# An opening written out by hand: the second tile's first projections, its input, the value weights and the key copies take other places

## The chip, the core and the metric

The kernel runs on one core of one Trainium2 chip. The engines are PE (TensorE, matrix products), DVE (VectorE), ACT (ScalarE), POOL (GpSimd) and SP (SyncE, which here only gives out DMA orders). The metric is device time in microseconds (us); lower is better. A measurement is the median of several runs, and one execution beside them is profiled.

## The reference, cut to what matters

```python
# x: (64, 32, 512); W: 16 matrices 32 x 32, one chosen for each batch
x = x + einsum('bct,bcd->bdt', x, W[condition])
# attention: 32 query heads, 8 key/value heads, D = 128, 32 new tokens a batch
q = rope(rmsnorm(x @ Wq.T), pos)      # 64 x 32 x 32 x 128
k = rope(rmsnorm(x @ Wk.T), pos)      # 64 x 32 x 8 x 128
v = x @ Wv.T
# 16 pages of 32 cached keys and values a batch, valid up to cache_seqlens
k_all = concat([k_cache[block_table], k]); v_all = concat([v_cache[block_table], v])
probs = softmax(where(valid, q @ k_all.T * SCALE, -1e30))
x = x + (probs @ v_all) @ Wo.T
```

All of it is float32. Each batch has 512 cached keys and 32 new ones; four query heads share one key head.

## The kernel before, in words

**Tiles and steps.** A tile is 128 rows: four batches of 32 tokens. There are 16 tiles, and the heads are done in two halves (four key heads and sixteen query heads each), so there are 32 steps. A step has 16 slots: four batches by four parts j. A part is one pair of key heads (g) by one half of the cached keys: j = 0 and 1 are the two pairs on the first half, j = 2 and 3 the two pairs on the second (`part_of`).

**What a tile needs.** `x1_a` (L383) loads the tile of x on SP's queue, `x1_c` (L404) multiplies it by the block matrix of its four mix weights (`bds`) and adds, `x1_b` (L411) transposes the sum on PE and has ACT copy it into `x1t`. A projection (`project`, L467) is four matmuls 128 x 512 from `x1t` and one weight tile, each shown as two records in the profile; `finish` squares it on ACT (L479), takes the power -1/2 on POOL (L487, L488), and scales and rotates it on DVE (`norm_rope`, L496 to L514). `q_a` and `k_a` are projection and finish, `q_b` and `k_b` transpose the rows on PE (L527) and have ACT copy them into `q_ring` (L611). `v_product` is the value projection (`pp_v`), `v_copy` its copy to `vn`. `rot_tables` (L454 to L459) makes a tile's cosines and sines times the norm weights, `reduced` (L141 to L152, DVE) and `sines` (L157 to L159, ACT) make the angles.

**What a batch needs.** `load_k` (L312) loads one key half: eight pages of 64 KB, eight orders on SP (L321). The halves lie in a ring of three buffers (tag `k_t`), so the fourth half can be asked for only when nothing reads the first one any more. `head_keys` (L1006) copies the pair of heads of part j out of its half into `kh` (four buffers and some spare places), on ACT (L1015) or on DVE (L1017). `scores` (L1020) multiplies keys and queries on PE and takes the exponential on ACT (L1037). `fetch` (L345) gathers value rows by an indirect DMA of POOL into a ring of three (L354), `fill` scales them into `v_ring` on ACT (L366). `values` (L1081) multiplies probabilities and values on PE (L1089) and, after the second half, adds and divides on DVE (L1100 to L1103).

**The order.** The opening (L1223 to L1335) is written by hand for all engines: each engine does its work in program order there. It holds the first tile's projections, the first batches' keys and values, the mix and `k_a` of the second tile, and the first batch of attention. Then a plan gives to each step and slot the work that is done beside the scores and values (L1340 on); step 0 holds the second tile's four query projections in slots 4 to 7 and its value projection in slot 13 (L1393 to L1404). SP and PE follow the program's order throughout.

**SP's queue in the opening.** x of the first tile, all mix weights (`w_all`), query weights 0 and 1, both key halves of batch 0, the value weights, x of the second tile, the second tile's mix weights (`load_cond_weights`, L284: a register load of the four numbers and four small DMAs), query weights 3, both key halves of batch 1, six output-weight parts (L262), two halves of batch 2, and then in step 0 x and mix weights of the third tile, six more output-weight parts and the halves that follow. Key weights and query weights 2 come on POOL's queue.

The ring of key halves in `load_k`, and the copy out of it in `head_keys`:

```python
k_raw = kv.tile([P, HP, GH, PSIZE], F32, tag="k_t", name=..., bufs=3)
for j in range(HP):
    nc.sync.dma_start(k_raw[:, j, :, :]..., kt[hh, bass.ds(page[half * HP + j], 1)]...)
...
g, half = part_of(ba, j)
src = ba.k_raw[half][:, :, g : g + 2, :]...
```

Of the kernel before, what the change touches and what calls it, by code (L numbers as in the profile page):

```python
# [12 lines left out]
F32 = mybir.dt.float32  # L13
I32 = mybir.dt.int32
AF = mybir.ActivationFunctionType
# [5 lines left out]
P = 128  # L21
# [7 lines left out]
BT = P // S  # L29
# [31 lines left out]
def cond_resid_paged_attention_kernel(  # L61
# [68 lines left out]
    def positions():  # L130
        nc.vector.memset(half_pi, math.pi / 2)
        nc.vector.memset(minus_half, -0.5)
        nc.vector.tensor_copy(pos, lens_sb)
        nc.vector.tensor_scalar(pos, pos, row, None, ALU.add)

    def reduced(t0, tmp):

        t1 = t0 + TRIG
        n = TRIG * HD
        ang, turns, red = (tmp[:, i, :] for i in range(3))  # L140
        nc.vector.tensor_tensor(  # L141
            ang.rearrange("p (t f) -> p t f", f=HD),
            freq.unsqueeze(1).to_broadcast([P, TRIG, HD]),
            pos[:, t0:t1].unsqueeze(2).to_broadcast([P, TRIG, HD]),
            ALU.mult,
        )
        nc.vector.tensor_scalar(turns, ang, 1.0 / TWO_PI, ROUND, ALU.mult, ALU.add)
        nc.vector.tensor_scalar(turns, turns, ROUND, None, ALU.subtract)
        nc.vector.scalar_tensor_tensor(red, turns, -C1, ang, ALU.mult, ALU.add)
        nc.vector.scalar_tensor_tensor(red, turns, -C2, red, ALU.mult, ALU.add)  # L150
        nc.vector.scalar_tensor_tensor(red, turns, -C3, red, ALU.mult, ALU.add)
        nc.vector.tensor_scalar(red, red, PI_IN, -PI_IN, ALU.min, ALU.max)  # L152

    def sines(trig, tmp):

        _, turns, red = (tmp[:, i, :] for i in range(3))
        nc.scalar.activation(trig[:, 1, :, :].rearrange("p t f -> p (t f)"), red, AF.Sin)  # L157
        nc.scalar.activation(turns, red, AF.Abs)
        nc.scalar.activation(  # L159
            trig[:, 0, :, :].rearrange("p t f -> p (t f)"),  # L160
            turns,
            AF.Sin,
            bias=half_pi,
            scale=-1.0,
        )
# [37 lines left out]
    def steps_of(exact, pools):  # L203
# [43 lines left out]
        def load_w(kind, hh, g=0, part=slice(0, 4), eng=nc.sync):  # L247
            if kind == "q":
                src = wq[:, (hh * QH + g * REP) * D : (hh * QH + (g + 1) * REP) * D]
            elif kind == "o":  # L250
                src = wo[(hh * QH + g * REP) * D : (hh * QH + (g + 1) * REP) * D, :]
            else:
                src = (wk if kind == "k" else wv)[:, hh * GH * D : (hh + 1) * GH * D]
            if part.start == 0:
                wt[kind, hh, g] = wpool.tile(
                    [P, 4, 512], F32, tag=f"w{kind}{g}", name=f"w{kind}{g}_{hh}_{uid}"
                )
            t = wt[kind, hh, g]
            if kind == "o" and not exact:
                src = src.rearrange("(h j p) e -> h p j e", h=REP, p=S)  # L260
                for h in range(part.start, part.stop):
                    nc.sync.dma_start(t[h * S : (h + 1) * S, :, :], src[h])  # L262
                return
            eng.dma_start(t[:, part, :], src.rearrange("(c p) e -> p c e", p=P)[:, part, :])
# [9 lines left out]
        def conditions(t, kind):  # L274
            _, number = nc.values_load_multi_w_load_instructions(
                cond_row[:, t, :],
                engines=[kind],
                min_val=0,
                max_val=NCOND - 1,
                skip_runtime_bounds_check_because="a batch's condition is one of those there are",  # L280
            )
            return number

        def load_cond_weights(t, eng=nc.sync, kind=mybir.EngineType.SP):  # L284
            number = conditions(t, kind)
            for i in range(BT):
                blk = slice(i * S, (i + 1) * S)
                eng.dma_start(
                    bds[t % 2][blk, blk],
                    w_cond.rearrange("(n s) e -> n s e", s=S)[bass.ds(number[i], 1)].rearrange(  # L290
                        "o s e -> (o s) e"
                    ),
                )
# [89 lines left out]
        def x1_a(st):  # L383

            if st.pair is None:
                tag = "sums" if st.n and not exact else "acc"
                st.acc = work.tile([P, HID], F32, tag=tag, name=f"acc_{st.name}", bufs=2)
            else:
                i = st.n % 2
                if i == 0:  # L390
                    st.pair.read = work.tile(
                        [P, 2, HID], F32, tag="os", name=f"read_{st.name}", bufs=1
                    )
                st.acc = st.pair.read[:, i]
            src = acc_d[st.t] if st.hh else x[st.t * P : (st.t + 1) * P, :]
            nc.sync.dma_start(st.acc, src)
# [14 lines left out]
        def x1_b(st):  # L411
            if st.hh:
                return
            pm = ps_p.tile([P, KC, P], F32, tag="pp", name=f"px1t_{st.name}")
            for c in range(KC):
                nc.tensor.transpose(pm[:, c, :], st.acc[:, c * P : (c + 1) * P], ident)
            if st.pair is None:
                st.x1t = work.tile(
                    [P, KC, P], F32, tag="x1t" if exact else "u3", name=f"x1t_{st.name}", bufs=1
                )  # L420
            nc.scalar.copy(st.x1t, pm)
            if st.n or exact:
                kept.append(lambda: keep_x1t(st, nc.sync))
# [195 lines left out]
        def k_b(st):  # L619
            to_columns(st, GH)  # L620
# [14 lines left out]
        def q_a(st, g):  # L635
            name = f"q_{st.name}_{g}"
            finish(st, g, project(st, wt["q", st.hh, g], f"pp_{name}"), name, "q")

        def q_b(st, g):
            to_columns(st, g)  # L640
# [584 lines left out]
        w_all = work.tile([S, NCOND, S], F32, tag="pr", name="w_all", bufs=2)  # L1225
        nc.sync.dma_start(w_all, w_cond.rearrange("(n s) e -> s n e", s=S))
        load_w("q", 0, 0)
        load_w("q", 0, 1)
        nc.scalar.dma_start(lens_sb, lens)
        load_w("k", 0, eng=nc.gpsimd)  # L1230
# [7 lines left out]
        load_w("q", 0, 2, eng=nc.gpsimd)  # L1238
        batch = Batch(first, 0)
        batch.load_half()  # L1240
        batch.load_half()
        load_w("v", 0)
        x1_a(second)
        def keep_warm(n):
            warm = ps_p.tile([P, P], F32, tag="pp", name="warm")
            for _ in range(n):
                nc.tensor.matmul(warm, ident, ident, start=True, stop=True)

        keep_warm(WARM)
        number = conditions(0, mybir.EngineType.DVE)  # L1250
        for i in range(BT):
            blk = slice(i * S, (i + 1) * S)
            nc.vector.tensor_copy(
                bds[0][blk, blk], w_all[:, bass.ds(number[i], 1), :].rearrange("p o e -> p (o e)")
            )
        x1_c(first)
        keep_warm(4)
        x1_b(first)
        keep_warm(3)
        load_cond_weights(1)  # L1260
        load_w("q", 0, 3)
        later = Batch(first, 1)
        later.load_half()
        positions()
        trig = work.tile([P, 3, TRIG * HD], F32, tag="w1", name="trig0", bufs=1)
        reduced(0, trig)
# [2 lines left out]
        nc.vector.memset(vn_bufs[0][:, :, D : D + 1], 1.0)  # L1269
        nc.vector.memset(vn_bufs[1][:, :, D : D + 1], 1.0)  # L1270
        cached_rows(pages_at, lens_at)
        trig = work.tile([P, 3, TRIG * HD], F32, tag="w1", name="trig1", bufs=1)
        reduced(TRIG, trig)
        q_a(first, 0)
        sines(new_trig(TRIG), trig)
        table = small.tile([P, 1], F32, tag="rs", name="table")
        nc.scalar.activation(table, half_pi, AF.Exp)
        fetch(0, 0)
        fetch(0, 1)
        k_a(first)  # L1280
# [1 line left out]
        keep_x1t(first, nc.gpsimd)  # L1282
        for kind in "qk":
            keep_rot(first, kind, nc.gpsimd)
        q_a(first, 1)
        q_a(first, 2)
        fetch(0, RAW, tag="pn", bufs=1)
        q_b(first, 0)
        head_keys(batch, 0, nc.scalar)
        head_keys(batch, 2, nc.scalar)  # L1290
        k_b(first)
        head_keys(batch, 1, nc.scalar)
        later.load_half()
        head_keys(batch, 3, nc.scalar)
        for part in (0, 1, 2):
            load_parts(outputs, 0, part)
        after = Batch(first, 2)
        after.load_half()
        new = v_product(first)
        q_b(first, 1)  # L1300
        scores(batch, 0)
        for c in (0, 1):
            batch.fill(c)
            fetch(1, c)
        v_copy(first, new)
        x1_c(second)
        batch.fill(2)
        fetch(1, 2)
        batch.fill(3)
        scores(batch, 2)  # L1310
        values(batch, 0)
        q_a(first, 3)
        q_b(first, 2)
        x1_b(second)
        keep_x1(second, nc.gpsimd)
        head_keys(later, 0, nc.scalar)
        head_keys(later, 1, nc.scalar)
        after.load_half()
        rot_tables(second)
        k_a(second)  # L1320
        q_b(first, 3)
        scores(batch, 1)
        scores(batch, 3)
# [68 lines left out]
        by_vector = nc.vector.tensor_copy  # L1392
        for kind in "qk":  # L1393
            at(0, 5, lambda kind=kind: keep_rot(second, kind))
        for g in range(GH):
            at(0, 4 + g, lambda g=g: q_a(second, g))
        at(0, 12, lambda: to_columns(second, GH), lambda: to_columns(second, 0, by_vector))
        at(0, 13, lambda: v_a(second), lambda: to_columns(second, 1, by_vector))
# [302 lines left out]
```

## Time and profile before

| what | us |
|---|---|
| runs shown | 2078.98, 2082.15, 2083.43; median 2082.15 |
| profiled execution | 2077.26, of it the span 2075.5 |
| PE busy in the span | 2042.3 (98%) |
| PE busy from 0 to 40 / 40 to 120 / 120 to 2000 / 2000 to 2075 | 30.0 / 75.9 / 1872.1 / 64.3 |
| value projection of the first tile (PE) | starts 32.92 |
| key projection of the second tile (PE) | starts 49.07 |
| query projections 0 and 1 of the second tile (PE) | start 63.05 and 68.37 |
| value weights (SP) | ordered at 24.43 |
| key halves of batch 0 in, first to last packet | 15.8 to 21.4 and 21.4 to 28.3 |
| key halves of batch 1 | 35.3 to 39.7 and 39.7 to 45.8 |
| key halves of batch 2 | 54.0 to 57.7 and 57.7 to 63.0 |
| key halves of batch 3 | 74.5 to 79.2 and 79.3 to 86.5 |
| key halves of batch 4 | 86.8 to 92.2 and 92.2 to 96.3 |

The profile is of one execution, and its times count from the start of the span. A line of a timeline gives start, duration, engine, line of the kernel, operation, output and input by the program's names, shapes and a count, and in brackets the idle time of the engine just before it with what ended it. A line of the waits gives the engine's operation, what it waited for, the sum, the number of times and the longest. SPq lines are DMA orders: from the first of a group to the last. The span's PE clock is full, except in a few short stretches.

### The profile page before, as it was taken

The numbers are of one execution on the slowest core, as the hardware profiler recorded it, in microseconds if no ns is written. First come the engines' busy times: TensorE is split into PE (matmuls) and PEld (weight loads), VectorE is DVE, ScalarE is ACT, GpSimd is POOL, SyncE is SP. The second block draws the span as 40 slices with busy tenths as digits, with TensorE's granted clock in tenths as the row PEclk, the third lists the DMA queues.
The fourth block names the chain that finished last, engine by engine and source line by source line (L and its number), as shares of the span: only waits on it lengthen the run. The fifth ranks groups of instructions, "written<-read, shape, count | busy, mean of one in ns | idle before, by whom it ended". The sixth has DMA issues, their size and how long they took to land.

```text
span 2075.5 us, 45239 instructions
## 1 busy us (share of the span) xinstructions
PE 2042.3 (98%) x13428; PEld 1587.7 (76%) x13428; DVE 1630.7 (79%) x3532; ACT 958.4 (46%) x2707; POOL 991.2 (48%) x1122
## 2 busy tenths in 40 slices
PE   7999999999999999999999999999999999999998
PEld 4767667787887878878786677878878787787886
DVE  4555687988979789797997769889797987979744
ACT  4444354544545444544534445344454434545441
POOL 4354465545636465463544436355353544535331
PEclk9999999999999999999999999999999999999999
DMA  8767557667676676787767876676767667676672
GB/s 245 202 177 219 160 153 230 183 190 220 186 218 188 195 215 189 220 264 217 222 193 201 241 212 184 201 207 179 209 184 211 188 195 211 178 215 182 191 212 78
DMA packets 410255, 413.33 MB, mean 199 GB/s; under 512 B 58928, under 2 KB 325552, under 8 KB 410000
## 3 DMA queue, kind: packets, MB, share of 16 engines
q1 hardware_dynamic: 354096, 229.87, 39.1%
q0 software_dynamic: 55168, 180.27, 28.9%
q8 instruction: 109, 1.79, 0.4%
q14 instruction: 146, 1.20, 0.2%
q10 hardware_dynamic: 736, 0.21, 0.0%
HBM read 350.09 MB, written 60.03 MB: 198 GB/s over the span
## 4 chain that ended last, share of the span: by engine, by line
PE 80%; DVE 6%; DMA 6%; SPq 4%; issue 2%; POOL 1%; ACT 1%; DVEq 0%; ACTq 0%; POOLq 0%
PE ps_x L1026 18%; PE po_x L1089 18%; PE p_x L836 14%; PE pb_x L697 8%; PE pc_x L697 6%; PE pa_x L697 6%; PE pout_x L793 4%; SPq L321 3%; DMA k_t_x<-in_kt_dram 2%; PE pnv_x L1071 2%; PE pp_q_x L470 2%; PE psn_x L1047 1%; DMA q_ring_x<-heads_d 1%; PE pp_v_x L470 1%; DMA wq_x<-in_wq_dram 1%
## 5 line engine op out<-in xcount | busy, mean ns | idle before, releaser
L354 POOL DMA_INDIRECT raw_x<-in_vc_dram,v_row x512 | 548.3, 1071 | 639.8 <-ACT v_ring_x L366 518.4
L1037 ACT ACTIVATE pr_x<-ps_x 128x512 f32<-128x512 f32 x511 | 305.7, 598 | 779.1 <-PE ps_x L1026 774.1
L1089 PEld LDWEIGHTS po_x<-v_ring_x,pr_x 128*128 128x128 f32 x4088 | 522.9, 191 | 86.8 <-issue 66.2
L1026 PE MATMUL ps_x<-q_ring_x,kh_x 128*128 128x128 f32 x4088 | 546.4, 276 | 1.6 <-ACT q_ring_x L611 1.6
L1089 PE MATMUL po_x<-v_ring_x,pr_x 128*128 128x129 f32 x4088 | 543.5, 275 | 3.2 <-DVE nv_x L1100 2.8
L1026 PEld LDWEIGHTS ps_x<-q_ring_x,kh_x 128*128 128x128 f32 x4088 | 498.7, 192 | 13.8 <-issue 3.1
L366 ACT ACTIVATE v_ring_x<-raw_x,valid 128x512 f32<-128x512 f32 x512 | 342.7, 714 | 19.8 <-DMA raw_x<-in_vc_dram,v_row 19.2
L1017 DVE COPY kh_x<-k_t_x 128x512 f32<-128x512 f32 x506 | 219.8, 435 | 97.6 <-PE ps_x L1026 67.2
L544 POOL DMA_DIRECT2D heads_d<-rows_x x150 | 126.2, 842 | 280.8 <-DVE rows_x L540 215.9
L697 PE MATMUL pb_x<-t_x,early 128*128 128x512 f32 x504 | 238.2, 595 | 2.0 <-DVE u_x L713 1.1
L1100 DVE TENSOR_TENSOR nv_x<-po_x,nv_x 128x258 f32<-128x258 f32 x256 | 106.9, 417 | 100.7 <-PE po_x L1089 96.1
L836 PEld LDWEIGHTS p_x<-wo_x,ot_x 128*128 128x128 f32 x624 | 116.5, 190 | 62.3 <-issue 45.9
L488 POOL TENSOR_TENSOR rs_q_x<-ms_q_x,minus_half 128x4 f32<-128x4 f32 x128 | 158.8, 1241 | 10.7
L836 PE MATMUL p_x<-wo_x,ot_x 128*128 128x256 f32 x624 | 156.3, 380 | 0.1
L836 PE MATMUL p_x<-ts_x,ot_x 128*128 128x256 f32 x624 | 145.6, 380 | 0.7 <-DVE ts_x L911 0.7
L697 PEld LDWEIGHTS pb_x<-t_x,early 128*128 128x128 f32 x504 | 86.2, 191 | 64.8 <-issue 61.9
L836 PEld LDWEIGHTS p_x<-ts_x,ot_x 128*128 128x128 f32 x624 | 115.4, 190 | 25.3 <-issue 8.4
L1103 DVE TENSOR_TENSOR nv_x<-nv_x,rden 128x256 f32<-128x256 f32 x256 | 109.6, 428 | 8.7
L479 ACT ACTIVATE sq_q_x<-u_x 128x128 f32<-128x128 f32 x224 | 66.2, 298 | 94.0 <-DVE u_x L713 94.0
L697 PE MATMUL pc_x<-wq_x,early 128*128 128x512 f32 x224 | 105.4, 593 | 0.0
L697 PE MATMUL pa_x<-wq_x,early 128*128 128x512 f32 x224 | 105.4, 593 | 0.0
L514 DVE TENSOR_TENSOR rope_q_x<-rope_q_x,rs_q_x 128x512 f32<-128x512 f32 x120 | 82.3, 686 | 19.8 <-POOL rs_q_x L488 19.3
(203 smaller groups left out, 2612.0 us busy)
## 6 DMA issues: line engine op xcount, KB each, us to landing
k_t_x<-in_kt_dram SPq DMA_DIRECT2D x2048, 64.0 KB
heads_d<-rows_x POOLq DMA_DIRECT2D x150, 256.0 KB
q_ring_x<-heads_d SPq DMA_DIRECT2D x480, 80.0 KB
raw_x<-in_vc_dram,v_row POOLq DMA_INDIRECT x512
wo_x<-in_wo_dram SPq DMA_DIRECT2D x32, 256.0 KB
res_x<-acc_d SPq DMA_DIRECT2D x31, 256.0 KB
wq_x<-in_wq_dram SPq DMA_DIRECT2D x8, 512.0 KB
early<-x1t_d SPq DMA_DIRECT2D x16, 256.0 KB
```

Source lines behind the costliest of these rows:

```text
L354: nc.gpsimd.indirect_dma_start(out=raw.rearrange("p g d -> p (g d)"), out_offset=None, in_=vc, in_offset=bass.IndirectOffsetOnAxis(ap=v_ro ...
L366: nc.scalar.activation(v_ring[:, c, :, 0:D], raw, AF.Copy, scale=valid[:, b, c : c + 1])
L488: nc.gpsimd.tensor_tensor(rs, ms, minus_half, ALU.pow)
L544: nc.gpsimd.dma_start(heads_d[st.n][:, :, i, :].rearrange("k p c -> p k c"), part)
L697: nc.tensor.matmul(bank, pair.x[:, i, c, :], by[:, c * 512 : (c + 1) * 512], start=start and c == 0, stop=c == 1, skip_group_check=not start,)
L836: nc.tensor.matmul(to, left[:, i, :], right(i), start=start and i == 0, stop=i == QH // 2 - 1, skip_group_check=True,)
L1017: nc.vector.tensor_copy(to, src)
L1026: nc.tensor.matmul(ps[:, c, i, :], ba.k[j][:, i, c, :], queries(ba, g + i), start=True, stop=True,)
L1037: nc.scalar.activation(pr, ps, AF.Exp, scale=SCALE)
L1089: nc.tensor.matmul(ba.po[g][:, i, :], ba.pr[j][:, c, i, :], ba.v_t[:, 2 * half + c, g + i, :], start=(half == 0 and c == 0 and i == 0), st ...
L1100: nc.vector.tensor_tensor(t, ba.po[g], t, ALU.add)
L1103: nc.vector.tensor_tensor(t[:, :, 0:D], t[:, :, 0:D], rd.unsqueeze(2).to_broadcast([P, 2, D]), ALU.mult,)
```

## The change

- x of the second tile is ordered on SP between query weights 0 and 1 (was: after both key halves and the value weights).
- The value weights are ordered between the two key halves of batch 0 (was: after both).
- The second tile's mix weights are picked by DVE out of `w_all`, as the first tile's are (was: four DMAs of SP).
- The second tile's mix follows the first query projection on PE, its transposes the second; its `x1t` lies in a second buffer of the tag `acc` (was: `u3`).
- Its `rot_tables` and `keep_x1` on POOL, its `k_a` and its `q_a` 0 come ahead of the value projection, its `q_a` 1 after the fourth query projection of the first tile. The plan of step 0 keeps `q_a` 2 and 3 in slots 6 and 7.
- The angles of tiles 2 and 3 (`trig1`, now tag `nv`), their sines and the load of the exponential's table come after the second tile's `q_a` 0 (was: around the first tile's `q_a` 0).
- ACT's key copies of batch 0: j = 0 after the second tile's `k_a`; j = 2 after the first scores (was: next to j = 0); j = 1 after the fourth query projection (was: after `k_b`); j = 3 after the column copy of q2, `q_b(first, 2)` (was: after j = 1).

The order on PE after it: mix and x1t of the first tile, q0, the second tile's mix, k, q1, the second tile's x1t, q2, transposes of q0 and k, k of the second tile, transposes of q1, q0 of the second tile, v, scores j = 0, scores j = 2, values j = 0, q3, transposes of q2, q1 of the second tile, transposes of q3, scores j = 1 and j = 3, then as before, less the two projections.

```diff
--- before.py
+++ after.py
@@ -415,8 +415,13 @@
             for c in range(KC):
                 nc.tensor.transpose(pm[:, c, :], st.acc[:, c * P : (c + 1) * P], ident)
             if st.pair is None:
+                tag = "x1t" if exact else "acc" if st.n == 1 else "u3"
                 st.x1t = work.tile(
-                    [P, KC, P], F32, tag="x1t" if exact else "u3", name=f"x1t_{st.name}", bufs=1
+                    [P, KC, P],
+                    F32,
+                    tag=tag,
+                    name=f"x1t_{st.name}",
+                    bufs=2 if tag == "acc" else 1,
                 )
             nc.scalar.copy(st.x1t, pm)
             if st.n or exact:
@@ -1225,6 +1230,7 @@
         w_all = work.tile([S, NCOND, S], F32, tag="pr", name="w_all", bufs=2)
         nc.sync.dma_start(w_all, w_cond.rearrange("(n s) e -> s n e", s=S))
         load_w("q", 0, 0)
+        x1_a(second)
         load_w("q", 0, 1)
         nc.scalar.dma_start(lens_sb, lens)
         load_w("k", 0, eng=nc.gpsimd)
@@ -1238,29 +1244,33 @@
         load_w("q", 0, 2, eng=nc.gpsimd)
         batch = Batch(first, 0)
         batch.load_half()
+        load_w("v", 0)
         batch.load_half()
-        load_w("v", 0)
-        x1_a(second)
         def keep_warm(n):
             warm = ps_p.tile([P, P], F32, tag="pp", name="warm")
             for _ in range(n):
                 nc.tensor.matmul(warm, ident, ident, start=True, stop=True)
 
         keep_warm(WARM)
-        number = conditions(0, mybir.EngineType.DVE)
-        for i in range(BT):
-            blk = slice(i * S, (i + 1) * S)
-            nc.vector.tensor_copy(
-                bds[0][blk, blk], w_all[:, bass.ds(number[i], 1), :].rearrange("p o e -> p (o e)")
-            )
+
+        def pick_weights(t):
+            number = conditions(t, mybir.EngineType.DVE)
+            for i in range(BT):
+                blk = slice(i * S, (i + 1) * S)
+                nc.vector.tensor_copy(
+                    bds[t][blk, blk],
+                    w_all[:, bass.ds(number[i], 1), :].rearrange("p o e -> p (o e)"),
+                )
+
+        pick_weights(0)
         x1_c(first)
         keep_warm(4)
         x1_b(first)
         keep_warm(3)
-        load_cond_weights(1)
         load_w("q", 0, 3)
         later = Batch(first, 1)
         later.load_half()
+        pick_weights(1)
         positions()
         trig = work.tile([P, 3, TRIG * HD], F32, tag="w1", name="trig0", bufs=1)
         reduced(0, trig)
@@ -1269,12 +1279,9 @@
         nc.vector.memset(vn_bufs[0][:, :, D : D + 1], 1.0)
         nc.vector.memset(vn_bufs[1][:, :, D : D + 1], 1.0)
         cached_rows(pages_at, lens_at)
-        trig = work.tile([P, 3, TRIG * HD], F32, tag="w1", name="trig1", bufs=1)
-        reduced(TRIG, trig)
-        q_a(first, 0)
-        sines(new_trig(TRIG), trig)
-        table = small.tile([P, 1], F32, tag="rs", name="table")
-        nc.scalar.activation(table, half_pi, AF.Exp)
+        pp = project(first, wt["q", 0, 0], "pp_q_first")
+        x1_c(second)
+        finish(first, 0, pp, f"q_{first.name}_0", "q")
         fetch(0, 0)
         fetch(0, 1)
         k_a(first)
@@ -1282,42 +1289,49 @@
         keep_x1t(first, nc.gpsimd)
         for kind in "qk":
             keep_rot(first, kind, nc.gpsimd)
-        q_a(first, 1)
+        pp = project(first, wt["q", 0, 1], "pp_q_first_1")
+        x1_b(second)
+        finish(first, 1, pp, f"q_{first.name}_1", "q")
+        trig = work.tile([P, 3, TRIG * HD], F32, tag="nv", name="trig1", bufs=1)
         q_a(first, 2)
         fetch(0, RAW, tag="pn", bufs=1)
+        keep_x1(second, nc.gpsimd)
+        rot_tables(second)
         q_b(first, 0)
+        k_b(first)
+        k_a(second)
         head_keys(batch, 0, nc.scalar)
-        head_keys(batch, 2, nc.scalar)
-        k_b(first)
-        head_keys(batch, 1, nc.scalar)
+        reduced(TRIG, trig)
+        q_b(first, 1)
+        q_a(second, 0)
+        sines(new_trig(TRIG), trig)
+        table = small.tile([P, 1], F32, tag="rs", name="table")
+        nc.scalar.activation(table, half_pi, AF.Exp)
         later.load_half()
-        head_keys(batch, 3, nc.scalar)
         for part in (0, 1, 2):
             load_parts(outputs, 0, part)
         after = Batch(first, 2)
         after.load_half()
         new = v_product(first)
-        q_b(first, 1)
         scores(batch, 0)
+        head_keys(batch, 2, nc.scalar)
         for c in (0, 1):
             batch.fill(c)
             fetch(1, c)
         v_copy(first, new)
-        x1_c(second)
         batch.fill(2)
         fetch(1, 2)
         batch.fill(3)
         scores(batch, 2)
         values(batch, 0)
         q_a(first, 3)
+        head_keys(batch, 1, nc.scalar)
         q_b(first, 2)
-        x1_b(second)
-        keep_x1(second, nc.gpsimd)
+        head_keys(batch, 3, nc.scalar)
+        q_a(second, 1)
         head_keys(later, 0, nc.scalar)
         head_keys(later, 1, nc.scalar)
         after.load_half()
-        rot_tables(second)
-        k_a(second)
         q_b(first, 3)
         scores(batch, 1)
         scores(batch, 3)
@@ -1392,7 +1406,7 @@
         by_vector = nc.vector.tensor_copy
         for kind in "qk":
             at(0, 5, lambda kind=kind: keep_rot(second, kind))
-        for g in range(GH):
+        for g in (2, 3):
             at(0, 4 + g, lambda g=g: q_a(second, g))
         at(0, 12, lambda: to_columns(second, GH), lambda: to_columns(second, 0, by_vector))
         at(0, 13, lambda: v_a(second), lambda: to_columns(second, 1, by_vector))
```

## The prediction

> **What bounds the kernel now.** I read the page first: busy time of the engines, then the waits of PE, then the timelines of the stretch that the change touches.
>
> ```profile
> PE 2042.3 (98%) x13428; PEld 1587.7 (76%) x13428; DVE 1630.7 (79%) x3532; ACT 958.4 (46%) x2707; POOL 991.2 (48%) x1122
> ```
>
> TensorE sets the time. PE idles 2075.5 - 2042.3 = 33.2 us, and the windows view says where: 14.1 of it in the first 120 us, 10.7 in the last 75, and only 7.9 between 120 and 2000. So what PE loses or gains in the opening stays to the end, as there is almost nothing later that could take it up. The waits of PE in the first 120 us (sum, times, longest):
>
> ```profile
> PE pp_v_x L470 <- DMA wv_x<-in_wv_dram: 3.5, 1, 3.5
> ...
> PE ps_x L1026 <- ACT q_ring_x L611: 1.6, 2, 1.2
> PE pp_k_x L470 <- ACT x1t_x L421: 1.5, 1, 1.5
> PE pp_q_x L470 <- DMA wq_x<-in_wq_dram: 1.3, 2, 0.8
> ```
>
> The largest is the wait for the value weights, and it costs more than its 3.5: the projection behind it is slow. PE's timeline and the windows (the value behind the five busy times is PE's clock, then the DMA share):
>
> ```profile
> 32.92 5.69 PE L470 MATMUL pp_v_x<-wv_x,x1t_x 128*128 128x512 f32 x8 [3.48 <-DMA wv_x<-in_wv_dram]
> ...
> 43.14 3.60 PE L470 MATMUL pp_q_x<-wq_x,x1t_x 128*128 128x512 f32 x8
> ```
> ```profile
> 30.00:35.00 5.00, 2.08 (x3) 1.08 (x4) 3.55 (x8) 3.64 (x14) 4.45 (x7) 0.52 0.95 337
> 35.00:40.00 5.00, 4.55 (x14) 2.20 (x14) 1.18 (x3) 1.12 (x3) 0.69 (x1) 0.80 0.80 261
> ```
>
> The clock was granted at half until about 37, so this projection took 5.69 where another took 3.60: about 2.0 more.
>
> **What the change takes away.** The value weights (512 KB) are asked for after the first key half and not after both. That half's last packet landed at 21.4 and the second half took until 28.3, so the weights land by an estimated 31. PE now reaches them later too: three steps of the second tile stand ahead of them. From the first query projection at 11.8, PE has six projections of 3.43 (one row's start to the next, 11.78 to 15.61 less the gap, and the x16 row of 7.10 for two), the mix 0.86, four groups of transposes at 0.44: 23.2, so 35.0, and 37.0 with the wait of the next part. The 3.48 and the 2.0 are gone. With them go the 1.46 for x1t and the 0.45 and 1.18 for q_ring, as these products are early. Added up, the most that can be won by slot 1 is 3.48 + 2.0 + 1.46 + 0.45 + 1.18 + some smaller ones = about 10.8.
>
> **What it adds for PE.** First, x of the second tile (256 KB) goes ahead of the second query weights on SP's queue. These landed at 20.04 with a wait of 0.76; at the 259 to 382 GB/s of 10 to 20 us, 256 KB are 0.7 to 1.0, bounds 0 (queues share the engines) and 2. I take 1.3, so PE waits 0.76 + 1.3 = about 2 there. Second, scores of j = 2 follow those of j = 0 on PE, but their key copy now stands behind the first exponential on ACT, itself behind the sines (1.0) and the table load (1.28). From the end of the first scores (41.2 to 41.9) that is 0.3 + 0.60 + 0.66, so PE waits 1.6, up to 3.6 if the sines are late. The DVE picks of the second mix weights are 4 x 0.17 = 0.7 (and register loads that no row of DVE shows: between 0, if hidden, and the 0.6 that SP stood before its own four at 26.10); they stand beside the wait for the angles, and the moved angle reduction gives 2.0 back ahead of the first rope. POOL's six products for the second tile's tables are 6 x 0.32 = 1.9, moved ahead of the power for k; POOL was free from 35.7 to 42.2, so nothing. SP loses four weight DMAs (3.55), also nothing: SP waits for landings there. Net gain of PE up to slot 1: about 3 to 5.
>
> **What it moves: the key copies.** This is what I think decides. Key halves come into a ring of three (k_t, L312); the half that follows may be asked for only when both copies out of the first one have been made. The first half is left by copies j = 0 and j = 1, the second by j = 2 and 3. Before, ACT made all four here:
>
> ```profile
> 32.84 1.17 ACT L1015 COPY kh_x<-k_t_x 128x512 f32<-128x512 f32 x2
> ...
> 34.35 0.66 ACT L1015 COPY kh_x<-k_t_x 128x512 f32<-128x512 f32 x1
> ```
>
> j = 1 was done at 35.0, well before SP came to the fourth half, whose first packet moved at 39.7. After the change j = 1 stands on ACT behind the squares of the fourth query projection of the first tile. PE does that one after the value projection (37.0 to 40.5), scores (0.9), the wait (1.6 to 3.6), scores and values (1.8) : 44.8 to 46.8, ends 48.2 to 50.2; 0.3 and 1.15 of squares and 0.66 for the copy make 50.3 to 52.3, and with a half clock behind one of the new waits about 2 later. I take 53, where it was 35.0. By PE's work alone, with no waits, it could not be before 49.
>
> SP takes its orders one after the other, so everything behind that half waits too:
>
> ```profile
> 31.95 11.26 SPq L321 DMA_DIRECT2D k_t_x<-in_kt_dram  x16
> 43.25 2.87 SPq L262 DMA_DIRECT2D wo_x<-in_wo_dram  x6
> 47.40 14.30 SPq L321 DMA_DIRECT2D k_t_x<-in_kt_dram  x16
> ...
> 85.80 24.02 SPq L321 DMA_DIRECT2D k_t_x<-in_kt_dram  x40
> ```
>
> From an order to its first packet an idle queue took 1.2 (132.32 to 133.52), so the fourth half starts at 54.2 and not 39.7: SP is 14.5 late. Some is made up, as the six output-weight parts of 256 KB took 8.2 (45.8 to 54.0) among other traffic: at the 262 GB/s of the first 40 us they are 6, so 2 back, with bounds of 0 and 7 (both groups of parts compressed). 12.5 late remain for the halves of batches 3 and 4.
>
> Had PE slack for that? At step 1 DVE was already waiting for keys, and its copies stand in order before work that PE needs:
>
> ```profile
> 94.09 0.43 DVE L1017 COPY kh_x<-k_t_x 128x512 f32<-128x512 f32 x1 [1.14 <-DMA k_t_x<-in_kt_dram]
> 94.49 0.29 DVE L611 COPY q_ring_x<-pt_x 128x128 f32<-128x128 f32 x1
> 94.69 0.55 DVE L613 COPY q_ring_x<-pt_x 128x384 f32<-128x384 f32 x1
> 95.16 0.42 DVE L1100 TENSOR_TENSOR nv_x<-po_x,nv_x 128x258 f32<-128x258 f32 x1
> ```
>
> Behind the sum at 95.16 (done 95.6) PE has a mix at 101.74 and values at 102.60, which need what DVE does there. From 95.6 to 102 is a slack of about 6.4. So PE is late by 12.5 - 6.4 = 6.1, whatever it won before: a win on PE of 3 to 5 makes it wait longer at that place and no more. Bounds: a copy at 51 is 12.5 late on SP, and with 7 made up that is 12.5 - 7 - 6.4 = -0.9 (nothing is late, and the win counts); at 55 with nothing made up, 16.5 - 6.4 = 10. After 110 each slot carries projections and key supply runs ahead of PE, so this is paid once.
>
> **The sum.** 2077.26, the profiled execution (span 2075.5 and 1.8 around it), plus 6.1 is 2083.4. The runs shown have a median of 2082.15, which is 4.9 above that execution; on their scale the forecast is 2088.
>
> [...] The row: the clock fell at 30.2, after waits of 1.23 and less than 1 us, and a half-clock window took 2.0 from PE. [...]
>
> **Rivals.**
> Faster: the ring's delay is hidden. Then the time is 2082 less 5 = 2077. It decides by when j = 1 is copied: up to 44.9 SP is at most 6.4 late and the slack takes all of it; up to 51 it does if SP makes up 7. For it: the ring copies ahead (batches 1 and 2 are loaded) may give more slack than the one row I used, and parts queued on SP may compress. Against it: 49 is the least PE's work allows.
> About the same, 2083 (2078 to 2086): the copy comes at 53 and SP makes up 5 to 7, which leaves 14.5 - 7 - 6.4 = 1 to 3 that PE loses, or the copy is early and the new waits eat most of the win.
> Worse, 2095: nothing made up (10) and one or two half-clock windows (2.0 each) in the long waits at 88 to 105.
> It doesn't do what it says: the value weights are still late, as they share the engines with the key halves; PE then waits near 37 as before, and the ring is later by that: 2091.
>
> **Chances.** Forecast 0.40, worse 0.09, not doing what it says 0.03: slower 0.52. About the same 0.28. Faster 0.20. About 0.2% (4.2 us) is what a measurement of this kernel can tell from no change. The range, 2077 to 2095, takes in the middle of the faster case and most of the worse one.
>
> **What would show it.** In the new trace: the wait for the value weights gone and their projection at 3.6; PE idle ahead of the second query weights about 2; the scores of j = 2 waiting for a key copy; ACT's copy for j = 1 at about 53; SP's fourth half starting there; PE waiting in 85 to 110 for DVE, with DVE waiting for k_t, 4 us or more in sum. If PE shows no such wait up to 120, my reason is wrong and the faster case holds.

## The result and the profile after

The changed kernel takes 2085.43 us (median of 22 runs, 2080.28 to 2089.45) and the kernel before 2080.95 (22 runs, 2074.89 to 2088.75). The ratio is 1.0026, with a 95% interval of 1.0017 to 1.0034: slower by about 5.4 us. The profiled executions are 2085.26 (span 2083.4) and 2077.26 (span 2075.5). The one of before is a quick one, 3.7 under its median, so the 7.9 between the two spans is more than the change costs.

The page of the changed kernel, then PE's waits in its first 120 us (sum, times, longest):

```profile
PE 2046.5 (98%) x13428; PEld 1594.3 (77%) x13428; DVE 1628.9 (78%) x3536; ACT 957.5 (46%) x2707; POOL 991.2 (48%) x1122
```
```profile
PE po_x L1094 <- DVE nv_x L1105: 4.2, 2, 3.0
PE px1t_x L416 <- DVE acc_x L409: 3.7, 1, 3.7
PE ps_x L1031 <- ACT kh_x L1020: 2.4, 1, 2.4
...
PE ps_x L1031 <- ACT q_ring_x L616: 1.7, 1, 1.7
...
PE pp_q_first L475 <- DMA wq_x<-in_wq_dram: 0.2, 1, 0.2
```

The wait for the value weights is gone. In its place stand one for a key copy of ACT, and 4.2 and 3.7 of waits for DVE (1.1 of the first kind before, none of the second). PE's timeline shows both, the good and the bad:

```profile
36.43 3.60 PE L475 MATMUL pp_v_x<-wv_x,x1t_x 128*128 128x512 f32 x8
39.86 1.05 PE L1031 MATMUL ps_x<-q_ring_x,kh_x 128*128 128x128 f32 x8
43.36 1.16 PE L1031 MATMUL ps_x<-q_ring_x,kh_x 128*128 128x128 f32 x8 [2.44 <-ACT kh_x L1020]
...
67.11 1.21 PE L1094 MATMUL po_x<-v_ring_x,pr_x 128*128 128x129 f32 x8
...
82.57 1.13 PE L1094 MATMUL po_x<-v_ring_x,pr_x 128*128 128x129 f32 x8 [1.14 <-DVE nv_x L1105]
...
87.63 1.13 PE L1094 MATMUL po_x<-v_ring_x,pr_x 128*128 128x129 f32 x8 [3.03 <-DVE nv_x L1105]
...
107.02 1.12 PE L416 MATMUL px1t_x<-ident,acc_x 128*128 128x128 f32 x4 [3.75 <-DVE acc_x L409]
```

The same two places in the kernel before:

```profile
71.80 1.05 PE L1089 MATMUL po_x<-v_ring_x,pr_x 128*128 128x129 f32 x8
...
104.38 0.60 PE L416 MATMUL px1t_x<-ident,acc_x 128*128 128x128 f32 x4
```

The value projection takes its 3.60 and does not wait. Values j = 0 of batch 1, with the same work done ahead of them in both kernels, come at 67.11 where they were at 71.80: PE has won 4.7. Then it waits three times. The first wait, 1.14, stands in the kernel before as well. The second, 3.03, takes most of the win: the scores at 102.22 are still 1.3 earlier than before (103.49). The third, 3.75, turns that into a loss: the transposes of the third tile, 104.38 before, are at 107.02. Behind these two waits lies the key supply. ACT's timeline (the copies j = 0, 2 and 1 of batch 0 in that order; j = 3 follows at 50.88) and SP's orders:

```profile
33.91 0.63 ACT L1020 COPY kh_x<-k_t_x 128x512 f32<-128x512 f32 x1
...
42.70 0.61 ACT L1020 COPY kh_x<-k_t_x 128x512 f32<-128x512 f32 x1
...
49.90 0.63 ACT L1020 COPY kh_x<-k_t_x 128x512 f32<-128x512 f32 x1
```
```profile
31.39 23.11 SPq L321 DMA_DIRECT2D k_t_x<-in_kt_dram  x16
```

The sixteen page orders of batch 1 took 11.26 of SP's time before and now take 23.11: SP stands in the middle of them, behind an order given at 36.24, until the copy j = 1 is done at 50.53; its next order comes at 50.55. From the packets of the key halves: the fourth half starts at 51.5 (39.7 before), and the last packets of the halves are late by 9.8 (batch 1), 8.1 and 7.9 (batch 2), 6.4 and 4.5 (batch 3), 5.0 and 6.0 (batch 4). DVE meets that here (its timeline, and the sum of its waits from 60 to 112):

```profile
97.93 0.43 DVE L1022 COPY kh_x<-k_t_x 128x512 f32<-128x512 f32 x1 [3.28 <-DMA k_t_x<-in_kt_dram]
...
104.62 0.43 DVE L1022 COPY kh_x<-k_t_x 128x512 f32<-128x512 f32 x1 [2.91 <-DMA k_t_x<-in_kt_dram]
...
106.28 0.68 DVE L409 TENSOR_TENSOR acc_x<-pmix_x,acc_x 128x512 f32<-128x512 f32 x1
```
```profile
DVE kh_x L1022 <- DMA k_t_x<-in_kt_dram: 10.1, 4, 3.3
```

It was 1.1 in the same stretch before. The key copy at 104.62 stands ahead of the sum of the mix, and that ahead of PE's transposes. In the kernel before, this copy waited for PE and not for keys, and the sum did not wait:

```profile
101.07 0.43 DVE L1017 COPY kh_x<-k_t_x 128x512 f32<-128x512 f32 x1 [0.41 <-PE ps_x L1026]
...
102.84 0.68 DVE L409 TENSOR_TENSOR acc_x<-pmix_x,acc_x 128x512 f32<-128x512 f32 x1
```

A wait put down to another transfer (rot_dq, 3.6 from 83.1 to 86.7) stands ahead of a key copy too, one that reads batch 3's first half, 6.4 late; PE's wait of 3.03 ends behind it. The windows show PE's clock around the long waits (the value behind the five busy times):

```profile
30.00:35.00 5.00, 5.00 (x16) 2.47 (x15) 3.69 (x9) 3.07 (x13) 4.62 (x10) 1.00 0.98 310
35.00:40.00 5.00, 5.00 (x14) 2.23 (x13) 4.66 (x13) 1.32 (x10) 2.86 (x5) 1.00 0.62 203
55.00:60.00 5.00, 4.40 (x47) 3.98 (x48) 1.80 (x4) 1.74 (x4) 0.47 (x1) 0.66 0.91 222
105.00:110.00 5.00, 2.98 (x14) 2.98 (x15) 2.48 (x9) 0.77 (x2) 1.80 (x2) 0.67 0.75 206
```

The half clock of before, 30 to 37, is gone, and there are two new stretches, 55.5 to 58.9 and 106.7 to 110.1. From one step's scores of the new keys to those of the next, PE is 4.1 late at 107 and the same 4.1 at 174 and 255: what was lost there was lost once. Of the rest of the 7.9, 2.2 came with a half-clock stretch at 1171.6 and 2.4 in the last 120 us; gains and losses between these (up to 1.5 each) take off a little under 1 in sum. Nothing that the change touches runs there, and the mean granted clock of the kernel before was anything from 0.992 to 0.998 in the 35 runs beside experiments 1 to 4, so I do not count them to the change. The 4.1 lie within the interval of the runs (3.5 to 7.1 us); where the rest of their 5.4 is lost, if anywhere, no profile shows.

### The profile page after: what moved, and what is told of

Read it like the earlier page. It is cut to its first block, busy times and chain, and to the rows that moved or that the text cites. A ratio compares the mean times of both kernels' runs of the same rounds, so it can differ in the third digit from the quotient of the medians.

```text
span 2083.4 us, 45235 instructions
## 1 busy us (share of the span) xinstructions
PE 2046.5 (98%) x13428; PEld 1594.3 (77%) x13428; DVE 1628.9 (78%) x3536; ACT 957.5 (46%) x2707; POOL 991.2 (48%) x1122
## 4 chain that ended last, share of the span: by engine, by line
PE 80%; DVE 6%; DMA 5%; SPq 3%; issue 3%; POOL 2%; ACT 1%; DVEq 0%; ACTq 0%; POOLq 0%
PE ps_x L1031 18%; PE po_x L1094 18%; PE p_x L841 14%; PE pb_x L702 9%; PE pc_x L702 6%; PE pa_x L702 6%; PE pout_x L798 4%; DMA k_t_x<-in_kt_dram 3%; SPq L321 2%; PE pnv_x L1076 2%; PE pp_q_x L475 1%; PE psn_x L1052 1%; DMA raw_x<-in_vc_dram,v_row 1%; DMA wq_x<-in_wq_dram 1%; DVE kh_x L1022 1%
## 5 line engine op out<-in xcount | busy, mean ns | idle before, releaser
L1105 DVE TENSOR_TENSOR nv_x<-po_x,nv_x 128x258 f32<-128x258 f32 x256 | 106.7, 417 | 106.0 <-PE po_x L1094 98.7
```

What stands on the lines that cost most here:

```text
L1105: nc.vector.tensor_tensor(t, ba.po[g], t, ALU.add)
```

## The experiments

Theory K is the one of the prediction: ACT's late key copies hold the ring, SP gets late, and DVE and then PE wait for keys. Its rivals say that PE's own new waits are the price (W), or that step 1 is limited by keys whatever PE wins (S). A ring of four buffers, the direct test, was not tried; the ring is tested through what empties it. Ratios are to the kernel before, measured beside each experiment.

**1. All four copies early.** The changed kernel, with j = 2, 1, 3 next to j = 0 in time:

```diff
         q_b(first, 1)
+        head_keys(batch, 2, nc.scalar)
+        head_keys(batch, 1, nc.scalar)
+        head_keys(batch, 3, nc.scalar)
         q_a(second, 0)
...
-        head_keys(batch, 2, nc.scalar)
...
-        head_keys(batch, 1, nc.scalar)
...
-        head_keys(batch, 3, nc.scalar)
```

> The changed kernel, with ACT's key copies j = 2, 1 and 3 of batch 0 put back to one place ahead of the value projection (behind the column copy of q1); all else as changed. Theory K (the late copies hold the ring of key halves, SP is late, DVE waits for keys between 82 and 107): the fourth half's first packet at 39 to 41 instead of 51.5, no wait of DVE for keys above 1.5 in 60 to 110, the transposes of the third tile on PE at 98 to 100 (changed 107.0, before 104.4), time 4 to 6 us below before, ratio 0.997 to 0.998. Rival W (PE's own new waits in 40 to 56 and the half clock behind them are the price, keys are not): only the wait of 2.4 for the key copy goes, so 2 to 3 below the changed kernel, ratio 1.001 to 1.002.

2077.36 (12 runs), ratio 0.9977 (0.9966 to 0.9987): faster than before, and its interval lies wholly below the changed kernel's (1.0017 to 1.0034); the medians are some 8 us apart. The fourth half starts at 37.9 (K said 39 to 41). SP's orders, and PE's largest waits in 120 us:

```profile
30.48 10.26 SPq L321 DMA_DIRECT2D k_t_x<-in_kt_dram  x16
```
```profile
PE po_x L1094 <- DVE nv_x L1105: 2.1, 1, 2.1
PE pmix_x L408 <- DVE bd L1260: 1.9, 1, 1.9
PE ps_x L1031 <- ACT q_ring_x L616: 1.7, 1, 1.7
PE po_x L1094 <- ACT v_ring_x L366: 1.7, 1, 1.7
```

SP's sixteen orders take 10.26 again and DVE has no listed wait for keys. The transposes of the third tile come at 101.0 (K said 98 to 100). W had 1.001 to 1.002 and falls.

**2. Only j = 1 and j = 3 early.** As the first, but j = 2 stays behind the first scores.

```diff
         q_b(first, 1)
+        head_keys(batch, 1, nc.scalar)
+        head_keys(batch, 3, nc.scalar)
         q_a(second, 0)
```

> The changed kernel, with only the copies j = 1 and j = 3 put ahead of the value projection; j = 2 stays behind the first scores, so PE's wait of 2.4 at 41 stays. j = 1 alone sets free the ring's first buffer. Theory K: the fourth half starts at 39 to 41, the third tile's transposes at 100 to 103, ratio 0.998 to 0.999. Rival W: as the changed kernel, ratio 1.002 to 1.003.

2077.70 (12 runs), ratio 0.9986 (0.9972 to 1.0000). PE's wait for the copy j = 2 is still there, even longer, and the scores behind it took 2.08, where those of j = 0 took 1.05:

```profile
43.70 2.08 PE L1031 MATMUL ps_x<-q_ring_x,kh_x 128*128 128x128 f32 x8 [3.23 <-ACT kh_x L1020]
```

Still the fourth half starts at 37.7, the third tile's transposes come at 102.8, and the median is 7.7 below the changed kernel's; the two intervals do not overlap. This is the cleanest separation: the visible new wait of PE was left in, the copies that free the ring were taken early, and the loss went.

**3. The kernel before, copies late.** One part of the change alone.

```diff
-        head_keys(batch, 1, nc.scalar)
         later.load_half()
-        head_keys(batch, 3, nc.scalar)
...
         q_a(first, 3)
+        head_keys(batch, 1, nc.scalar)
         q_b(first, 2)
+        head_keys(batch, 3, nc.scalar)
```

> The kernel before, with the copies j = 1 and j = 3 alone moved late, j = 1 behind the fourth query projection and j = 3 behind the column copy of q2, as the change has them. Theory K: copy j = 1 done at about 48.5, the fourth half's first packet at about 49.5 (before 39.7), waits of DVE for keys between 82 and 107, and the third tile's transposes 0.5 to 3 later than before's 104.4; ratio 1.000 to 1.0015, less than the change's loss, since PE here has not run ahead and there is no half-clock stretch at 107. Rival W: nothing moves, ratio 1.000, transposes at 104.4.

2081.96 (12 runs), ratio 0.9997 (0.9984 to 1.0011), an interval that takes in both expectations. The fourth half started at 50.1, but DVE waited only 1.5 for keys. PE in this profile was already 3.3 late at 56, for another reason, and the same 3.3 late at 107: its projection of the second tile's keys waited 2.5 for the copy x1t, where it waited 1.5 before. The late key copies stood ahead of that copy on ACT, and the projection then took 5.40, where it took 3.70 before. A PE that comes late does not have to wait for late keys. So the run told nothing apart, and experiment 8 repeats it without that.

**4. The kernel before, SP's orders changed.** x of the second tile and the value weights early, nothing else.

```diff
         load_w("q", 0, 0)
+        x1_a(second)
         load_w("q", 0, 1)
...
         batch.load_half()
+        load_w("v", 0)
         batch.load_half()
-        load_w("v", 0)
-        x1_a(second)
```

> The kernel before, with only SP's orders changed: x of the second tile between query weights 0 and 1, value weights between the key halves of batch 0. Theory K: the wait for the value weights falls from 3.5 to below 1 and their projection takes 3.6 to 3.9, PE is 3 to 5 earlier at slot 1 (values j = 0 of batch 1 at 67 to 69, before 71.8), ring as before, ratio 0.998 to 0.999. Rival S (supply of keys sets step 1, whatever PE wins before it): PE is earlier in the opening, but waits for DVE between 82 and 107 by as much, ratio 0.9995 to 1.0005.

2078.71 (12 runs), ratio 0.9987 (0.9972 to 1.0002). The value projection, on PE's timeline:

```profile
30.90 3.67 PE L470 MATMUL pp_v_x<-wv_x,x1t_x 128*128 128x512 f32 x8 [1.36 <-DVE ropeu_q_x L504]
```

No wait for weights, and 3.67 for the projection that took 5.69 before. The third tile's transposes come at 100.8, 3.5 earlier than before, and DVE waits 0.8 for keys. So S falls by the trace; by the runs alone it would not, as their interval reaches 1.0002. This is as early as in experiment 1 (101.0), which does the second tile's projections early as well: up to this point, in these two profiles, the order of SP wins by itself all that the change wins with early key copies. The runs, 0.9987 and 0.9977, do not tell the two apart.

**5. Copies early, and q3's column copy early.** On top of experiment 1, aimed at the 1.7 in its list.

```diff
+        q_b(first, 3)
         head_keys(later, 0, nc.scalar)
         head_keys(later, 1, nc.scalar)
         after.load_half()
-        q_b(first, 3)
```

> The first experiment (copies j = 2, 1 and 3 early) and the column copy of q3 on ACT ahead of the two key copies of batch 1, which made the scores j = 1 wait 1.7 for it. Theory K: that wait falls below 0.7, 1 us off the first experiment at step 1, ratio 0.997. A rival: step 1 is held by the sum of rows on DVE (the wait of 2.1 at 82) or by keys, and nothing is left of it, 0.9977.

2073.10 (7 runs), ratio 0.9965 (0.9950 to 0.9980), the fastest kernel here. The wait fell to 0.6, but in the profile, which is of its longest run (2079.46), PE is at the same place at 107 as in experiment 1 (3.4 earlier than before), since another wait grew:

```profile
82.10 1.13 PE L1094 MATMUL po_x<-v_ring_x,pr_x 128*128 128x129 f32 x8 [3.27 <-DVE nv_x L1105]
```

So the rival fits the trace and K's number fits the runs; the intervals of the two experiments overlap. On ACT, the squares of the second tile's third projection there stand behind the scaling of value rows that had waited 6.83 for their gather. That this gather is the next limit is read from the trace and was not tried.

**6. Angles early too.** On top of experiment 5.

```diff
         k_b(first)
+        reduced(TRIG, trig)
+        sines(new_trig(TRIG), trig)
+        table = small.tile([P, 1], F32, tag="rs", name="table")
+        nc.scalar.activation(table, half_pi, AF.Exp)
         k_a(second)
```

> The kernel of the experiment before it (copies early, q3's column copy early), and the angles, sines and the table load of the exponential put ahead of the second tile's key projection, so that the first exponential does not stand behind them. Theory K: the wait of 1.7 of the values j = 0 for the value rows goes, 1 to 1.7 less again, ratio 0.996 to 0.997, if the angle reduction on DVE ahead of the norm of k does not make PE wait elsewhere. Rival: it does (squares and rope of the second tile 2 later, the copy j = 1 at 40), and nothing is won, 0.997 to 0.998.

2081.41 (11 runs), ratio 1.0003 (0.9989 to 1.0017): the win is gone, as the rival said, and more: the rival had 0.997 to 0.998. PE's timeline:

```profile
46.84 2.06 PE L1094 MATMUL po_x<-v_ring_x,pr_x 128*128 128x129 f32 x8 [3.94 <-DVE v_ring_x L371]
```

ACT now does the sines and the table ahead of the squares of k, so DVE waits 3.6 for these, its norms of k and of the second tile's q0 end at 46.5, and a small copy of the validity column stands in order behind them. PE's values j = 0, which need it, start at 46.84, where they started at 44.03 in experiment 5; they took 2.06 and the fourth projection behind them 5.32, where it was 1.32 and 3.60. The angles were in the way on either side, and here they held DVE's work too.

**7. Projections back in their slots.** The changed kernel without the early `q_a` 0 and 1 of the second tile.

```diff
-        q_a(second, 0)
...
-        q_a(second, 1)
...
-        for g in (2, 3):
+        for g in range(GH):
```

> The changed kernel with the second tile's query projections 0 and 1 back in slots 4 and 5 of step 0; copies, SP's orders and k_a of the second tile as changed. Theory K: the fourth query projection comes earlier, but less than the 3.4 taken out ahead of it, since the first exponential waits for the sines: copy j = 1 done at 47 to 48.5, fourth half's first packet at 48 to 49.5 (changed 51.5), third tile's transposes at 104 to 106 (changed 107.0), ratio 1.000 to 1.0015. Rival W (the moved projections are what costs): ratio 0.998 to 0.999.

2085.76 (12 runs), ratio 1.0020 (1.0008 to 1.0033). Both expectations missed. The scores j = 2 waited far longer:

```profile
43.60 2.08 PE L1031 MATMUL ps_x<-q_ring_x,kh_x 128*128 128x128 f32 x8 [6.41 <-ACT kh_x L1020]
```

The projection that I took out ahead of the scores had filled the time in which ACT waits for the angles; the key copy j = 2 ended at 43.5, as in the changed kernel (43.3), the fourth projection, behind that wait, took 4.46 (3.60 in the changed kernel), and j = 1 was done at 53.3, not at 47 to 48.5. The fourth half started at 54.3 and DVE waited 10.2 for keys. So W falls again: with the projections back in their slots the loss is still there. PE is 5.5 late at 107 in this profile, 4.1 in the changed kernel's; in the runs the two intervals overlap.

**8. The kernel before, copies behind batch 1's.** Experiment 3 repaired: ACT's x1t copy comes first.

```diff
         head_keys(later, 0, nc.scalar)
         head_keys(later, 1, nc.scalar)
+        head_keys(batch, 1, nc.scalar)
+        head_keys(batch, 3, nc.scalar)
```

(and the two copies taken out where they were)

> The kernel before, with the copies j = 1 and j = 3 behind the key copies of batch 1 on ACT, so that they do not stand ahead of the second tile's x1t copy as in the third experiment. Theory K: PE is as before up to 85 (slot 1 within 0.5 of 71.8), the copy j = 1 is done at 50.7, the fourth half starts at 51 to 52, the key halves of batch 4 land at 97 to 103, DVE waits for keys in 82 to 107, and the third tile's transposes come at 106 to 107.5 (before 104.4), as in the changed kernel, since the keys' own time sets it: 1.001. Rival W: nothing moves after 60, transposes at 104.4, ratio 1.000.

2082.56 (12 runs), ratio 1.0007 (0.9994 to 1.0021). DVE's waits from 60 to 112, and the third tile's transposes on PE's timeline:

```profile
DVE kh_x L1017 <- DMA k_t_x<-in_kt_dram: 11.7, 5, 4.6
```
```profile
108.24 0.65 PE L416 MATMUL px1t_x<-ident,acc_x 128*128 128x128 f32 x4 [2.53 <-DVE acc_x L409]
```

The fourth half started at 52.7, batch 4's halves landed at 98.9 and 103.6, and the wait of the transposes for the sum of the mix, which the kernel before does not have, is here with nothing else of the change done. PE was 1.2 late at 56 (before the keys matter) and 3.9 at 107. PE was not as before up to 85, as K had said: the 1.2 come from the value projection, which took 6.68 and not 5.69, and the transposes are that much later than the 106 to 107.5 of K. The late copies alone make the waits; the time itself, +1.5, is not clear of no change. So the trace shows that the late copies are enough to make the waits, and experiments 1 and 2 show in the time that the loss goes with them.

## Why the prediction was right, point by point

The forecast was +0.29%, and +0.26% was measured, by the mechanism it named: the late copy held the ring, SP stood, and DVE and then PE waited for keys. That the number came out so close is luck, as its terms were less good than its sum:

- **Value weights.** Wait 3.48 and half clock 2.0 gone: so it was (36.43, 3.60). Their size was misread: they are 1024 KB in the list of transfers and not 512. PE came to them so late that this cost nothing.
- **q_ring.** The forecast let the waits for q_ring (0.45 and 1.18) go. They did not: 1.67 in one wait is left at 55.6, and the half clock from 55.5 to 58.9 stands behind it.
- **Second query weights.** Forecast a wait of 2, measured 0.21. The weights came only 0.8 later, and PE reached them later too, as the mix of 0.86 stands ahead and PE's first projection began at 12.63 and not 11.78.
- **Scores j = 2.** Forecast 1.6 to 3.6, measured 2.44.
- **Win up to slot 1.** Forecast 3 to 5, measured 4.7.
- **Copy j = 1.** Forecast 53, measured 50.5, within the 50.3 to 52.3 worked out before I added 2 for a half clock that did not come.
- **SP.** The fourth half 14.5 late by the forecast, 11.8 measured. I let SP make up 2, and it made up 5.8 (11.8 less the 6.0 of batch 4's second half), inside the bounds 0 to 7. The fourth half itself came in 4.1 and not 6.1, and the gaps ahead of the halves of batches 2 and 3, in which other transfers run, fell from 8.2 and 11.5 to 6.4 and 9.4.
- **Slack.** Forecast 6.4, measured 3.4 (6.0 late at the half, 107.02 - 104.38 = 2.6 late on PE). This is the term that was read off the wrong place. I took the copy at 94.09, since it was the one that already waited for a transfer. The one that binds is the next half's: it landed at 96.3, its copy at 101.07 had less room, and the sum of the mix at 102.84 is followed by PE's transposes at 104.38.
- **12.5 - 6.4 = 6.1** was thus in truth 6.0 - 3.4 = 2.6, and 1.5 from the half clock at 106.7, which I had left at nothing: 4.1 at 107. Two sizes, each nearly twice too large, cancelled in part. This is the luck: SP made up 5.8, within the 5 to 7 that the rival "about the same" asked for, and with the slack of 6.4 that I had read, 6.0 late at the half would have cost nothing.
- **Half clock.** The forecast priced a half clock only in the copy j = 1 and none in PE's sum. Two came: the one at 106.7 stands behind a wait of 3.75, the one at 55.5 behind waits of 1.67 and 0.35.
- **Waits in 85 to 110**: 4 or more was forecast, and 3.03 + 3.75 = 6.8 measured.

The rivals: the faster case needed the copy by 44.9 or 7 made up. It is what experiments 1, 2 and 5 are, with the copy j = 1 done at 35.7 to 36.8: there the change's other parts win 3 to 7 us.

## What to carry to other kernels

When a ring of buffers is filled by one engine's queue, the last reader of a buffer is part of that queue: before moving a copy later, look up which order waits for its buffer and what stands behind that order, not only who needs the copy's output. A stall that such a move makes can show up far away (here 34 and 53 us behind the copy, on DVE and PE), and its price here was the lateness that was left there less the slack of the work that stands behind it in order (2.6), with 1.5 of a half clock on top, so look for the place with the least slack, not for the first one that waits. And split a change that does several things: here the whole without the late copies is at 0.9977, and with them at 1.0026.

## What the runs showed of the hardware

In the trace of the kernel before, PE's granted clock was half from 30.16 to 36.98 and from 2071.33 to the end; in that of the changed kernel from 55.46 to 58.88, 106.66 to 110.08, 1171.62 to 1175.03, 2011.30 to 2014.71 and from 2079.57 to the end. Each of these stretches that ended took 3.41, the first 6.83, which is two of it, and the 47.79 of full clock between 58.88 and 106.66 are 14 of it. In the 3.41 us ahead of each fall PE was idle for 1.95 and 2.35 (before) and for 1.89, 3.39, 1.44, 2.38 and 2.60 (changed).

Idle time did not always bring a fall: 1.82 in the 3.41 us from 2003.06 on (before) and 1.67 in those from 2014.71 on (changed) were followed by full clock, though 1.44 ahead of 1171.62 was followed by half. The changed kernel's wait of 3.03 at 84.6, 1.58 idle from 82.77 to 86.18 and 1.45 from there to 89.59, cost no clock (1.00 in both and behind them). The clock came back to full behind half-clock stretches with 0 to 0.43 of idle PE, and stayed at half behind the 3.41 us from 30.16 on with 2.76 (before). In experiment 1 the values and scores behind a wait of 2.10 at 82.09 took 1.86 and 1.92, where those ahead of it took 1.06.
